# Perceiver kernel on one core: biases added to x ahead, a shorter last layernorm, fewer count matmuls, logits behind each tile's transposes, last value scaling shared

## The chip, the cores and the metric

The kernel runs on one core of a Trainium2 chip. The metric is the device time of one execution in microseconds (us). All data is float32.

## The reference, cut to what matters

x has 256 rows of 512, the context 25088 rows of 512. Six residual blocks follow each other; LN is a layernorm without scale.

```python
x = x + (LN(x) @ W1.T + mean(ctx @ W2.T) + b)                  # L0 cross
x = x + windowed_causal_attention(LN(x)) @ Wo.T + bo           # L0 attention, 16 heads
x = x + moe16(LN(x))               # sigmoid scores, groups, top 4 of 16 experts + a shared one
x = x + cross_attention(LN(x), ctx) @ Wo + bo                  # L1 cross, softmax over the QUERIES
x = x + shifted_window_attention(LN(x)) @ w_o + b_o            # L1 attention, windows of 128, shift 64
# L1 FFN: top 2 of 8 experts
logits = (LN(x) @ gate_w + gate_b) / 0.9
probs  = softmax(logits where among the top 2)
out    = sum_e probs[:, e] * (gelu(LN(x) @ w1[e] + b1[e]) @ w2[e] + b2[e])
x = x + (out - mean(out)) / sqrt(var(out) + eps) * ln_g + ln_b
```

The softmax of the L1 cross attention runs over the 256 queries, so each context row has its own sum per head; the kernel divides the values V by these sums.

## The kernel before, in words

x lies in SBUF as [128 partitions, T=2 tiles, 512]. The L1 cross attention is nearly the whole time: 49 chunks of 512 context rows are turned into K and V by products of sums of blocks (L537, with sums by POOL at L523 and additions into kT and v by DVE at L559), then for each chunk and 128 rows come scores (L1021), maxima (L1030), exponentials (L1035), sums inverted (L1056), V scaled (L1062, on POOL) and attend (L1048). K and V depend only on the context, so this work also serves as fill: while the blocks before it leave TensorE idle, `early_fill` makes chunks ahead and keeps them in SBUF or sends them to HBM. The chunks are also summed for the mean of the L0 cross block.

What sets the order: instructions written as `queue << ...` keep the program's order on their engine. All others are placed by a scheduler that works with a model of times and priorities, so where an addition on DVE ends up is seen in the built program only. Tiles come from pools; a pool gives addresses, and a DMA into an address that other tiles had before waits for their last readers. SP issues most DMAs in its own order; POOL issues a few.

The names that matter:

- `norm_T` (L166): per tile of x, `norm_stats` (L154: bn_stats, bn_aggr, sqrt on ACT, reciprocal), xn (L172), four transposes on TensorE (L179), one or two copies into xT (L182, L184).
- `add_rows` (L187): a bias row block `rows[row]` is added to a result in PSUM into a tile `tmp` (L190), and then `tmp` to x (L191). Called by `project_out` (L208) for the three attention outputs, by the L0 cross block (L686) and by the last layernorm.
- L0 cross: weights `l0x_w` loaded at L670, `l0a_wo` at L671, `cmean_b` is the mean of the context, 32 matmuls at L684. L0 attention (`self_attention`, L218) loads `l0a_wqkv` at L690 and uses it at L198 and L233.
- `places_of` (L453): counts, by matmuls with a triangular matrix `low` and with `ones`, how many rows ahead chose the same expert. Called by both expert blocks.
- `all_logits` (L465): the gate's matmuls (L469), after norm_T is done with both tiles.
- L1 attention: `window_attention` (L315), with q and k (L330, copies out at L336 to L340), scores (L351), project_out (L212). The rows of biases used late are loaded at L1144 (DMA at L100).
- L1 FFN (from L1156): logits in `lg` (L1169), scaled (L1170), `rank_of`, keep, counts, the list of items (expert and up to 128 rows), whose experts' numbers reach registers by `expert_i` (L1200) and start the weights' DMAs (L1214). `run_items` (L1301) goes through 8 items and then, under an If, more. An item has 4 parts (hf) of 512 hidden units; each does 16 matmuls (L1332, two records each in the profile), gelu on ACT (L1338), and, one part later, the second product (L1312). `weights_and_rows` (L1262) makes the softmax weights, the bias rows' product (L1274, L1277) and the scatter matrices (L1282 to L1285); it is called in item 0 behind the first part's gelu.
- The last layernorm (from L1367) normalises the two tiles of y in PSUM, multiplies by ln_g, adds ln_b and x, and writes x out (L1373).

Of the kernel before, what the change touches and what calls it, by code (L numbers as in the profile page):

```python
# [9 lines left out]
F32 = mybir.dt.float32  # L10
AF = mybir.ActivationFunctionType
ALU = mybir.AluOpType
# [25 lines left out]
def perceiver_kernel(  # L38
# [32 lines left out]
    def ps_mm(shape=None):  # L71
        tile, home = take("mm", shape)
        give(home)
        return tile
# [3 lines left out]
    def ps_ac(shape=None):  # L78
        return psum.tile(shape or [P, 512], F32, tag="ac", name="ps_ac", bufs=2)
# [83 lines left out]
        nc.vector.reciprocal(rs, sd)  # L163
        return mv[:, 0:1], rs

    def norm_T(roll=0, fill=None, untransposed=None):  # L166

        xT = work.tile([P, DC, NT], F32, tag="xT", name="xT", bufs=1)
        for t in range(T):
            mean, rs = norm_stats(x[:, t, :])  # L170
            xn = work.tile([P, D], F32, tag="xn", name="xn")
            nc.vector.tensor_scalar(xn, x[:, t, :], mean, rs, ALU.subtract, ALU.mult)  # L172
            if untransposed is not None:
                untransposed.append(xn)
            if t == 0 and fill:
                fill(2)
            tp = ps_mm([P, DC, P])
            for dc in range(DC):
                queue << nc.tensor.transpose(tp[:, dc, :], xn[:, dc * P : (dc + 1) * P], ident)  # L179
            at = (t * P - roll) % NT  # L180
            first = min(P, NT - at)
            nc.vector.tensor_copy(xT[:, :, at : at + first], tp[:, :, :first])  # L182
            if first < P:
                nc.vector.tensor_copy(xT[:, :, : P - first], tp[:, :, first:])  # L184
        return xT

    def add_rows(t, ps, row):  # L187

        tmp = work.tile([P, D], F32, tag="tmp", name="tmp")
        nc.vector.tensor_add(tmp, ps, rows[row])  # L190
        nc.vector.tensor_add(x[:, t, :], x[:, t, :], tmp)  # L191

    def feature_major(res, w, xT, col, scale=None):

# [10 lines left out]
            else:  # L205
                nc.vector.tensor_scalar(res[:, fc, :], ps, b, scale, ALU.add, ALU.mult)

    def project_out(oT, w, row):  # L208
        for t in range(T):
            ps = ps_mm()  # L210
            for dc in range(DC):
                queue << nc.tensor.matmul(  # L212
                    ps, oT[:, dc, t * P : (t + 1) * P], w[:, dc, :],
                    start=dc == 0, stop=dc == DC - 1,
                )
            add_rows(t, ps, row)

    def self_attention(xT, wo, col_q, row_v, row_o, blocks, load_qkv, fill):  # L218

        with tc.tile_pool(name="sa", bufs=1) as sa:  # L220
            v = sa.tile([P, T, D], F32, name="v_sa")
            oT = sa.tile([P, DC, NT], F32, name="oT")
            qT = sa.tile([P, DC, NT], F32, name="qT_sa")
            kT = sa.tile([P, DC, NT], F32, name="kT_sa")
            with tc.tile_pool(name="saw", bufs=1) as saw:
                wqkv = load_qkv(saw)
                xT = xT()
                feature_major(qT, wqkv[0], xT, col_q)
                feature_major(kT, wqkv[1], xT, col_q + 1)
                for t in range(T):  # L230
                    ps = ps_mm()
                    for dc in range(DC):
                        queue << nc.tensor.matmul(  # L233
                            ps, xT[:, dc, t * P : (t + 1) * P], wqkv[2][:, dc, :],
                            start=dc == 0, stop=dc == DC - 1,
                        )
                    nc.vector.tensor_add(v[:, t, :], ps, rows[row_v])
            with tc.tile_pool(name="sas", bufs=2) as sas:
                attention_blocks(sas, qT, kT, v, oT, blocks, fill)
            fill(1)  # L240
            project_out(oT, wo, row_o)

    def attention_blocks(sas, qT, kT, v, oT, blocks, fill):
        def weights(t, qp):
# [70 lines left out]
    def window_attention(xT, wqkv, wo, col_q, row_v, row_o):  # L315
# [6 lines left out]
        with tc.tile_pool(name="wa", bufs=1) as wa, tc.tile_pool(name="was", bufs=2) as was:  # L322
# [93 lines left out]
            for t in range(T):  # L416
                ps = ps_mm()
                for dc in range(DC):
                    queue << nc.tensor.matmul(
                        ps, xT[:, dc, t * P : (t + 1) * P], wv[:, dc, :],  # L420
                        start=dc == 0, stop=dc == DC - 1,
                    )
                nc.vector.tensor_add(v[:, t, :], ps, rows[row_v])
                for b in range(2):
                    nc.sync.dma_start(
                        out=v_swapped[b * HT : (b + 1) * HT, t, :],
                        in_=v[(1 - b) * HT : (2 - b) * HT, t, :],
                    )
            pT0 = transposed(e0)
            pT1 = transposed(e1)  # L430
            attend(0, pT0)
            attend(1, pT1)
            project_out(oT, wo, row_o)

    def rank_of(pool, vals, shape):

# [15 lines left out]

    def places_of(pool, chosen, n):  # L453

        ps = ps_mm([P, T + 1, n])
        for k, terms in enumerate((((low, 0),), ((ones, 0), (low, 1)), ((ones, 0), (ones, 1)))):
            for m, (w, t) in enumerate(terms):
                queue << nc.tensor.matmul(
                    ps[:, k, :], w, chosen[:, t, :], start=m == 0, stop=m == len(terms) - 1
                )  # L460
        count = pool.tile([P, T + 1, n], F32, name="count", bufs=1)
        nc.vector.tensor_copy(count, ps)
        return count[:, :T, :], count[:, T, :]

    def all_logits(xT, w, n):  # L465
        ps = ps_mm([P, T, n])
        for t in range(T):
            for dc in range(DC):
                queue << nc.tensor.matmul(  # L469
                    ps[:, t, :], xT[:, dc, t * P : (t + 1) * P], w[:, dc, :],  # L470
                    start=dc == 0, stop=dc == DC - 1,
                )
        return ps

    ps = ps_mm([P, P])
    queue << nc.tensor.matmul(ps, ones, low, start=True, stop=True)
# [191 lines left out]
    with tc.tile_pool(name="l0xw", bufs=1) as l0xw:  # L668
# [8 lines left out]
        nc.vector.tensor_copy(cmean_b, cmean.unsqueeze(2).to_broadcast([P, DC, P]))  # L677

        xT = norm_T()
        pss = [ps_mm() for _ in range(T)]  # L680
        for k in range(2 * DC):
            for t in range(T):
                lhsT = xT[:, k, t * P : (t + 1) * P] if k < DC else cmean_b[:, k - DC, :]
                queue << nc.tensor.matmul(pss[t], lhsT, l0x_w[:, k, :], start=k == 0, stop=k == 2 * DC - 1)  # L684
        for t in range(T):
            add_rows(t, pss[t], R_L0X_B)  # L686

    def l0a_qkv(pool):
        w = pool.tile([P, DC, 3 * D], F32, name="l0a_wqkv")
# [16 lines left out]
    NDENSE = (4 * NT) // (P + 1)  # L706
    NSPARSE = NE0 - NDENSE
    xns = []
    xT = norm_T(fill=early_fill, untransposed=xns)
    TE = [P, T, NE0]  # L710
    ps = all_logits(xT, l0g_w, NE0)

    def mini(shape, name, dtype=F32):
        return moe0.tile(shape, dtype, name=name, bufs=1)
# [207 lines left out]
    with tc.tile_pool(name="xa", bufs=2) as xa:  # L922
# [73 lines left out]
        def fill(upto):  # L996
            nonlocal done
            while done < min(upto, total):
                for _ in range(groups[done % len(groups)]):
                    next(stream)  # L1000
                done += 1

        fill(5)
        qT = xa.tile([P, DC, NT], F32, name="qT", bufs=1)
        feature_major(qT, wq, norm_T(fill=lambda n: fill(7)), C_L1X_BQ, SCALE)
        acc = [ps_ac([P, 2, NT]) for _ in range(2)]

        def restore(c):
# [47 lines left out]
            queue << nc.vector.reciprocal(rc, sm.rearrange("p q r -> p (q r)"))  # L1056
            return rc

        def scaled(c, s, rc):

            vs = xa.tile([P, D], F32, tag="vs", name="vs", bufs=3)
            queue << nc.gpsimd.tensor_mul(  # L1062
                vs.rearrange("p (h d) -> p h d", h=H),
                vs_of[c, s].rearrange("p (h d) -> p h d", h=H),
                rc.unsqueeze(2).to_broadcast([P, H, HD]),
            )
            return vs


# [47 lines left out]
                pending = ((n == 2, n == halves_of), [es, None], [c, s, sm])  # L1117
            finished(c)
        pc, ps, psm = pending[2]
        pending[1][1] = scaled(pc, ps, inverse(psm))  # L1120
        attend(*waiting.pop())
        for qp in range(2):
            attend(*pending[0], qp, *pending[1])
# [12 lines left out]
        oT = xa.tile([P, DC, NT], F32, tag="oT", name="oT", bufs=1)  # L1136
        for qp in range(2):
            queue << nc.vector.tensor_copy(oT[:, 2 * qp : 2 * qp + 2, :], acc[qp])
        project_out(oT, wo, R_L1X_BO)
    ctx_scope.close()  # L1140


# [13 lines left out]
    experts = ExitStack()  # L1156
    ep = experts.enter_context(tc.tile_pool(name="experts", bufs=2))
    xns = []
    xT = norm_T(untransposed=xns)
    y = [ps_ac() for _ in range(T)]  # L1160

    def mini(shape, name, dtype=F32):
# [1 line left out]


    TE = [P, T, NE1]
    ps = all_logits(xT, l1g_w, NE1)
    lg = mini(TE, "lg")
    nc.vector.tensor_add(lg, ps, grow[:, NE0:].unsqueeze(1).to_broadcast(TE))  # L1169
    nc.vector.tensor_scalar(lg, lg, 1.0 / 0.9, None, ALU.mult)  # L1170
    rank = rank_of(ep, lg, TE)
    keep = mini(TE, "keep")
    nc.vector.tensor_scalar(keep, rank, 2.0, None, ALU.is_lt)
# [48 lines left out]

    ex, nm, sm = mini(TE, "ex"), mini([P, T], "nm1"), mini([P, T], "sm1")
    nc.vector.tensor_reduce(nm, lg, AX.X, ALU.max, negate=True)
    for t in range(T):
        nc.scalar.activation(ex[:, t, :], lg[:, t, :], AF.Exp, bias=nm[:, t : t + 1])
    place = mini(TE, "place")
    nc.vector.scalar_tensor_tensor(
        place, before.unsqueeze(1).to_broadcast(TE), float(P), places, ALU.mult, ALU.add
# [30 lines left out]
    rows_of = mini([P, 2, 2, T, P], "rows_of")  # L1260

    def weights_and_rows():  # L1262
        nc.vector.tensor_mul(ex, ex, keep)
        nc.vector.tensor_reduce(sm, ex, AX.X, ALU.add)
        nc.vector.reciprocal(sm, sm)
# [35 lines left out]
    def run_items(which, final):  # L1301
# [21 lines left out]
        for item in which:  # L1323
# [3 lines left out]
            for hf, wt in enumerate(parts):  # L1327
# [9 lines left out]
                for fc in range(FC):  # L1337
                    nc.scalar.activation(  # L1338
                        hT[:, fc, :], ps[:, fc, :], AF.Gelu, bias=b1[:, hf * FC + fc : hf * FC + fc + 1]
                    )  # L1340
                if pending is None and which[0] == 0:
                    weights_and_rows()
                if hf == NHF - 1 and item + 1 in which:
                    xg = gathered(item + 1)
# [22 lines left out]
    for t in range(T):  # L1367
        mean, rs = norm_stats(y[t])
        yn = work.tile([P, D], F32, tag="xn", name="yn")
        nc.vector.tensor_scalar(yn, y[t], mean, rs, ALU.subtract, ALU.mult)  # L1370
        nc.vector.tensor_mul(yn, yn, rows[R_LN_G])  # L1371
        add_rows(t, yn, R_LN_B)
        nc.sync.dma_start(out=out_v[:, t, :], in_=x[:, t, :])  # L1373
    experts.close()
    ffn_scope.close()
# [73 lines left out]
```

## Time and profile before

| what | us |
|---|---|
| three runs | 2798.63, 2798.04, 2798.18; median 2798.18 |
| the profiled execution: its time | 2799.3 |
| its span | 2797.6 |
| mean granted clock of TensorE | 0.987 |
| TensorE's wait at L737 for the first experts' weights, at 344.34 | 6.28 |
| TensorE's wait at L198 for l0a_wqkv, at 220.68 | 3.39 |

In the profile a row of the timeline has its start, its length, engine, line, operation, tiles, and in brackets the idle time before it and what ended that. A row "x16" holds 16 instructions of one kind in a run. PE is TensorE, PEld its weight loads, DVE VectorE, ACT ScalarE, POOL GpSimd, SP SyncE. A row of the waits has the engine and line that waited, what it waited for, the total, the number of times and the longest. PEclk in tenths is the clock that TensorE was granted.

### The profile page before, as it was taken

To read this page: it belongs to the slowest core of one execution; us is meant where nothing else is said; L and a number is where in the kernel's file an instruction comes from. 1 tells how busy PE (TensorE), PEld (TensorE's weight loads), DVE (VectorE), ACT (ScalarE), POOL (GpSimd) and SP (SyncE) were. 2 spreads that over 40 slices of the span, in tenths; PEclk is the share of its full clock that TensorE was granted. 3 is DMA by queue.
4 is the path that set the end of the run, shared out by engine and by line. 5 is a ranking of instruction groups with operands and counts; after the bars stand their busy time and mean duration, and the time that the engine had idled before them with its cause. 6 is when DMAs were issued, how large, how long until landed. Compare 5 with 4: busy or idle time off the path is not lost. (4 is left out here: it accounts for less than half of the span.)

```text
span 2797.6 us, 57238 instructions
## 1 busy us (share of the span) xinstructions
PE 2721.9 (97%) x21502; PEld 1920.9 (69%) x21502; DVE 1721.7 (62%) x3052; ACT 1700.9 (61%) x7001; POOL 577.5 (21%) x529
## 2 busy tenths in 40 slices
PE   8998899999999999999999999999999999979997
PEld 7866777776666666666666666666666666656775
DVE  4436512267777777777777777777777777742101
ACT  6832100037877777777777778777887778831111
POOL 4321000023222223222222232222222323100000
PEclk9999999999999999999999999999999999989999
DMA  9961344421100101000101000101000100107673
GB/s 387 423 266 76 134 160 170 162 91 41 37 32 32 41 22 47 32 32 32 46 17 47 32 32 32 46 17 47 32 32 32 47 17 27 51 24 297 259 271 145
DMA packets 40869, 262.87 MB, mean 94 GB/s; under 512 B 5320, under 2 KB 8440, under 8 KB 13200
## 3 DMA queue, kind: packets, MB, share of 16 engines
q1 hardware_dynamic: 37408, 237.85, 22.6%
q0 software_dynamic: 3184, 21.33, 1.9%
q8 instruction: 175, 2.87, 0.4%
q14 instruction: 102, 0.84, 0.1%
HBM read 239.23 MB, written 19.40 MB: 92 GB/s over the span
## 5 line engine op out<-in xcount | busy, mean ns | idle before, releaser
L1035 ACT ACTIVATE e<-ps_sc,nm 128x256 f32<-128x256 f32 x3136 | 1437.8, 485 | 377.4 <-DVE nm L1030 376.9
L1030 DVE TENSOR_REDUCE nm<-ps_sc 128x2 f32<-128x512 f32 x1568 | 995.3, 686 | 358.0 <-PE ps_sc L1021 357.9
L1035 ACT ACTIVATION_READ_ACCUMULATOR e<-ps_sc,nm 128x1 f32 x3136 | 678.7, 216 | 0.0
L1048 PE MATMUL ps_ac<-e,vs 128*32 128x256 f32 x6272 | 420.7, 386 | 4.1 <-POOL vs L1062 4.1
L537 PE MATMUL ps_kv<-ts,wq 128*128 128x256 f32 x1568 | 387.1, 391 | 5.8 <-POOL ts L523 5.8
L537 PE MATMUL ps_kv<-wq,ts 128*128 128x256 f32 x1568 | 388.8, 392 | 0.0
L1062 POOL TENSOR_TENSOR vs<-v,rc 128x512 f32<-128x512 f32 x160 | 167.8, 1049 | 1016.3 <-DVE rc L1056 1016.3
L537 PEld LDWEIGHTS ps_kv<-ts,wq 128*128 128x128 f32 x1568 | 286.1, 190 | 91.1 <-issue 27.3
L537 PEld LDWEIGHTS ps_kv<-wq,ts 128*128 128x128 f32 x1568 | 287.2, 191 | 85.2 <-issue 26.5
L1021 PE MATMUL ps_sc<-qT,kT 32*128 32x256 f32 x4096 | 304.1, 401 | 1.5 <-ACT e L1035 1.3
L1048 PEld LDWEIGHTS ps_ac<-e,vs 128*32 128x32 f32 x6272 | 164.2, 109 | 202.2 <-issue 114.1
L559 DVE TENSOR_TENSOR v<-v,ps_kv 128x512 f32<-128x512 f32 x343 | 227.7, 677 | 82.6 <-PE ps_kv L537 58.1
L1021 PEld LDWEIGHTS ps_sc<-qT,kT 32*128 32x128 f32 x4096 | 191.4, 184 | 116.5 <-ACT e L1035 106.4
L537 PE MATMUL ps_kv<-wq,ct 128*128 128x256 f32 x1008 | 244.2, 385 | 0.0
L537 PE MATMUL ps_kv<-ct,wq 128*128 128x256 f32 x1008 | 242.4, 383 | 0.0
L559 DVE TENSOR_TENSOR kT<-kT,ps_kv 128x512 f32<-128x512 f32 x280 | 187.1, 681 | 68.4 <-PE ps_kv L537 58.4
L537 PEld LDWEIGHTS ps_kv<-wq,ct 128*128 128x128 f32 x1008 | 189.7, 191 | 38.2 <-ACT e L1035 12.9
L537 PEld LDWEIGHTS ps_kv<-ct,wq 128*128 128x128 f32 x1008 | 188.1, 190 | 38.1 <-ACT e L1035 12.6
L1338 ACT ACTIVATE hT<-ps_mm,b 128x128 f32<-128x128 f32 x128 | 36.6, 368 | 210.5 <-PE ps_mm L1332 157.3
L1021 PE MATMUL ps_sc<-qT,kTp 32*128 32x256 f32 x2176 | 156.9, 400 | 0.0
L523 POOL TENSOR_TENSOR ts<-ct 128x512 f32<-128x512 f32 x84 | 107.1, 1275 | 230.9 <-DMA ct<-in_ctx_dram 230.9
L1021 PEld LDWEIGHTS ps_sc<-qT,kTp 32*128 32x128 f32 x2176 | 99.6, 184 | 58.7 <-ACT e L1035 55.2
(273 smaller groups left out, 2180.2 us busy)
## 6 DMA issues: line engine op xcount, KB each, us to landing
ct<-in_ctx_dram SPq DMA_DIRECT2D x67, 1024.0 KB, 5.0
we<-in_l1e_dram SPq DMA_DIRECT2D x64, 1024.0 KB, 6.8
we<-in_l0e_dram SPq DMA_DIRECT2D x17, 1536.0 KB, 8.1
cs<-in_ctx_dram SPq DMA_DIRECT2D x17, 1024.0 KB, 14.6
we0o<-in_l0e_dram SPq DMA_DIRECT2D x17, 768.0 KB, 4.5
kv<-kT POOLq DMA_DIRECT2D x9, 1024.0 KB, 9.7
kv<-v POOLq DMA_DIRECT2D x9, 1024.0 KB, 9.4
vp<-kv SPq DMA_DIRECT2D x9, 1024.0 KB, 4.8
```

The costliest lines, as they stand in the source:

```text
L523: queue << nc.gpsimd.tensor_sub(ts[:, k], a, b)
L537: queue << nc.tensor.matmul(ps[:, m, :], fixed[:, d, m * P : (m + 1) * P], moving[:, d, :], start=d == 0, stop=d == 1,)
L559: queue << nc.vector.tensor_tensor(to, old, ps, ALU.subtract if a == W_A22 else ALU.add)
L1021: queue << nc.tensor.matmul(sc[r][:, i, :], kTs[c][part, 2 * qp + i, s * P : (s + 1) * P], qT[part, 2 * qp + i, :], start=True, stop=True,)
L1030: queue << nc.vector.tensor_reduce(nm[:, 2 * qp : 2 * qp + 2, r], sc[r], AX.X, ALU.max, negate=True)
L1035: queue << nc.scalar.activation(e[:, 4 * i + r, :], sc[r][:, i, :], AF.Exp, bias=nm[:, q, r : r + 1], accum_out=sm[:, q, r : r + 1],)
L1048: queue << nc.tensor.matmul(acc[qp][32 * r : 32 * r + 32, i, :], v[:, h * HD : (h + 1) * HD], es[qp][:, 4 * i + r, :], start=first and i = ...
L1062: queue << nc.gpsimd.tensor_mul(vs.rearrange("p (h d) -> p h d", h=H), vs_of[c, s].rearrange("p (h d) -> p h d", h=H), rc.unsqueeze(2).to_ ...
L1338: nc.scalar.activation(hT[:, fc, :], ps[:, fc, :], AF.Gelu, bias=b1[:, hf * FC + fc : hf * FC + fc + 1])
```

## The change

Bias rows are added to x on their own, each as soon as x's old value has been read (`add_row`), and project_out and the L0 cross block add the result in PSUM to x directly; `tmp` is gone. The last layernorm is two operations a tile. The counts take two matmuls with both tiles side by side, and two additions. In the L1 FFN the gate's matmuls of a tile stand behind that tile's transposes, the factor 1/0.9 moves from the logits into the exponential and its maximum, and `weights_and_rows`, which adds ln_b to x as well, is called behind the gelu of item 0's second part. The last of the value scalings is divided by heads between DVE and POOL.

```diff
-    def norm_T(roll=0, fill=None, untransposed=None):
+    def norm_T(roll=0, fill=None, untransposed=None, then=None):
...
+            if then is not None:
+                then(xT, t)
         return xT
 
-    def add_rows(t, ps, row):
-
-        tmp = work.tile([P, D], F32, tag="tmp", name="tmp")
-        nc.vector.tensor_add(tmp, ps, rows[row])
-        nc.vector.tensor_add(x[:, t, :], x[:, t, :], tmp)
+    def add_row(row):
+
+        for t in range(T):
+            nc.vector.tensor_add(x[:, t, :], x[:, t, :], rows[row])
...
-    def project_out(oT, w, row):
+    def project_out(oT, w):
...
-            add_rows(t, ps, row)
+            nc.vector.tensor_add(x[:, t, :], x[:, t, :], ps)
...
                     nc.vector.tensor_add(v[:, t, :], ps, rows[row_v])
+            add_row(row_o)
...
+            add_row(row_o)
             pT0 = transposed(e0)
             pT1 = transposed(e1)
             attend(0, pT0)
             attend(1, pT1)
-            project_out(oT, wo, row_o)
+            project_out(oT, wo)
...
-        ps = ps_mm([P, T + 1, n])
-        for k, terms in enumerate((((low, 0),), ((ones, 0), (low, 1)), ((ones, 0), (ones, 1)))):
-            for m, (w, t) in enumerate(terms):
-                queue << nc.tensor.matmul(
-                    ps[:, k, :], w, chosen[:, t, :], start=m == 0, stop=m == len(terms) - 1
-                )
-        count = pool.tile([P, T + 1, n], F32, name="count", bufs=1)
+        ps = ps_mm([P, 2, T, n])
+        for k, w in enumerate((low, ones)):
+            queue << nc.tensor.matmul(ps[:, k], w, chosen, start=True, stop=True)
+        count = pool.tile([P, 2, T, n], F32, name="count", bufs=1)
         nc.vector.tensor_copy(count, ps)
-        return count[:, :T, :], count[:, T, :]
+        place, total = count[:, 0], pool.tile([P, n], F32, name="total", bufs=1)
+        assert T == 2
+        nc.vector.tensor_add(total, count[:, 1, 0, :], count[:, 1, 1, :])
+        nc.vector.tensor_add(place[:, 1, :], place[:, 1, :], count[:, 1, 0, :])
+        return place, total
...
         xT = norm_T()
+        add_row(R_L0X_B)
...
-            add_rows(t, pss[t], R_L0X_B)
+            nc.vector.tensor_add(x[:, t, :], x[:, t, :], pss[t])
...
         feature_major(qT, wq, norm_T(fill=lambda n: fill(7)), C_L1X_BQ, SCALE)
+        add_row(R_L1X_BO)
...
-        def scaled(c, s, rc):
+        def scaled(c, s, rc, engines=(nc.gpsimd,)):
 
             vs = xa.tile([P, D], F32, tag="vs", name="vs", bufs=3)
-            queue << nc.gpsimd.tensor_mul(
-                vs.rearrange("p (h d) -> p h d", h=H),
-                vs_of[c, s].rearrange("p (h d) -> p h d", h=H),
-                rc.unsqueeze(2).to_broadcast([P, H, HD]),
-            )
+            n = H // len(engines)
+            for k, engine in enumerate(engines):
+                heads = slice(k * n, (k + 1) * n)
+                queue << engine.tensor_mul(
+                    vs.rearrange("p (h d) -> p h d", h=H)[:, heads],
+                    vs_of[c, s].rearrange("p (h d) -> p h d", h=H)[:, heads],
+                    rc[:, heads].unsqueeze(2).to_broadcast([P, n, HD]),
+                )
             return vs
...
-        pending[1][1] = scaled(pc, ps, inverse(psm))
+        pending[1][1] = scaled(pc, ps, inverse(psm), engines=(nc.vector, nc.gpsimd))
...
-    xT = norm_T(untransposed=xns)
+    ps, make = logits(l1g_w, NE1)
+    xT = norm_T(untransposed=xns, then=make)
...
-    ps = all_logits(xT, l1g_w, NE1)
     lg = mini(TE, "lg")
     nc.vector.tensor_add(lg, ps, grow[:, NE0:].unsqueeze(1).to_broadcast(TE))
-    nc.vector.tensor_scalar(lg, lg, 1.0 / 0.9, None, ALU.mult)
...
     nc.vector.tensor_reduce(nm, lg, AX.X, ALU.max, negate=True)
+    nc.vector.tensor_scalar(nm, nm, 1.0 / 0.9, None, ALU.mult)
     for t in range(T):
-        nc.scalar.activation(ex[:, t, :], lg[:, t, :], AF.Exp, bias=nm[:, t : t + 1])
+        nc.scalar.activation(ex[:, t, :], lg[:, t, :], AF.Exp, bias=nm[:, t : t + 1], scale=1.0 / 0.9)
...
     def weights_and_rows():
+        add_row(R_LN_B)
...
-                if pending is None and which[0] == 0:
+                if item == 0 and hf == 1:
                     weights_and_rows()
...
-        nc.vector.tensor_scalar(yn, y[t], mean, rs, ALU.subtract, ALU.mult)
-        nc.vector.tensor_mul(yn, yn, rows[R_LN_G])
-        add_rows(t, yn, R_LN_B)
+        nc.vector.scalar_tensor_tensor(yn, y[t], mean, rows[R_LN_G], ALU.subtract, ALU.mult)
+        nc.vector.scalar_tensor_tensor(x[:, t, :], yn, rs, x[:, t, :], ALU.mult, ALU.add)
         nc.sync.dma_start(out=out_v[:, t, :], in_=x[:, t, :])
```

`logits(w, n)` makes the PSUM tile and returns with it a function `make(xT, t)` with one tile's four matmuls of `all_logits`; in the L0 block it is called for both tiles behind `norm_T`, as before.

## The prediction

> **What bounds the kernel now.** I read the page's engine shares and slices first, then the PE rows of the waits, then the timeline around each stall.
>
> ```profile
> PE 2721.9 (97%) x21502; PEld 1920.9 (69%) x21502; DVE 1721.7 (62%) x3052; ACT 1700.9 (61%) x7001; POOL 577.5 (21%) x529
> ...
> PE   8998899999999999999999999999999999979997
> ...
> PEclk9999999999999999999999999999999999989999
> ```
>
> TensorE is busy 97% of the span. Asked by stretches, it is busy for 150 of 150 us in 850 to 1000 and for all of 1000 to 2400, where the change touches nothing: the built order of every engine and its waits are the same there before and after. What the change can win lies in the other 76 us, where TensorE stands still or runs at a lower granted clock, and in the tail after its last matmul. PE's waits:
>
> ```profile
> PE ps_mm L179 <- DVE xn L172: 6.7, 3, 2.5
> PE ps_mm L476 <- POOL low L128: 6.1, 1, 6.1
> PE ps_kv L537 <- POOL ts L523: 5.8, 2, 5.4
> PE ps_mm L684 <- issue: 5.3, 1, 5.3
> PE ps_ac L1048 <- POOL vs L1062: 4.1, 1, 4.1
> ```
>
> The columns are total, times, longest. The first, fourth and fifth are touched. The fourth names no releaser, so I asked the timeline and SP's own waits:
>
> ```profile
> SPq L670 <- PE ps_kv L537: 19.4, 1, 19.4
> ```
>
> ```profile
> 185.06 0.33 SPq L670 DMA_DIRECT2D l0x_w<-in_l0x_w_dram  x1
> ...
> 192.81 9.83 PE L684 MATMUL ps_mm<-l0x_w,xT 128*128 128x512 f32 x16 [5.28 <-issue]
> ...
> 202.47 7.03 PE L684 MATMUL ps_mm<-l0x_w,cmean_b 128*128 128x512 f32 x16
> ```
>
> The weights of the first projection are asked for at 185.06, after SP has waited 19.4 us for a matmul on the memory they go to. By the DMA issues (2048 KB, 7.5 us to landing) they are there at 192.56, and TensorE starts at 192.81. The two groups of 16 are alike, yet the first takes 2.8 us more: the granted clock is 0.50 in 192 to 198.
>
> **The change, part by part.** All against the profiled run: 2799.3 us, span 2797.6. The median of the runs is 2798.18, 1.1 lower; I apply the difference to it.
>
> *The tile tmp goes.* Its two buffers of 2 KB a partition free room, so addresses move. In the built order, l0x_w's DMA stands behind the last cs load, ahead of l0a_wo (issued at 151.35), and has no wait at all. At the 423 GB/s of that stretch its 2 MB take 5.0 us and land near 165. TensorE can then start L684 once xT is copied: the copies run from 187.29 to 188.57, so at about 188.3 instead of 192.81, −4.5. The idle before it is then about 0.8 us, the clock should hold, and the first group takes 7.0 instead of 9.8: −2.8. Together −7.3. Cover: the two ct loads behind it land at about 176 instead of 171; POOL reads them at about 180.65. Without those 5 us of slack the price would be up to 5. The next load, l0a_wqkv (L690), still waits for the last L684 matmul and takes 11.0 us, so TensorE's 3.39 us wait at 220.68 stays. The clock held there; moved to another moment it may not (the same loss, 2.8, at an estimated chance of 1 in 7): +0.4.
>
> *Biases ahead.* project_out makes one addition per tile from PSUM instead of two operations; ten separate additions of 0.69 on DVE take their place. The first two come at about 25 us, behind the first fill's additions on DVE; they wait for the first rows, issued by POOL at 6.38 and landed at about 14.4, so nothing stands behind them. Those of L0 attention and L1 cross attention fall among fill work, where TensorE has queued matmuls and DVE is busy 62% of the span: 0 for all six (up to 0.7 each where a full PSUM ring makes TensorE wait). In window attention they stand ahead of the first qT_wa on DVE, which was idle 3.87 us before it: 0. They do wait for the rows' DMA there (last rival). R_LN_B's two sit inside the FFN norm and are counted there.
>
> *Counts.* Five matmuls become two; an f32 matmul shows as two records, so ten become four. For L0 (L458, 329.87 to 331.06) six at 0.12 are −0.7, and two more DVE additions at 0.2 are +0.4. They lead through expert_i to the experts' weights, for which TensorE waits 6.28 us at 344.34; the clock's phase after that wait is unknown: −0.3, between −1 and +0.7.
>
> *Last value scaling shared.*
>
> ```profile
> 2450.15 0.25 DVE L1056 RECIPROCAL rc<-sm 128x16 f32<-128x16 f32 x1 [2.29 <-ACT e L1035]
> 2450.57 1.05 POOL L1062 TENSOR_TENSOR vs<-v,rc 128x512 f32<-128x512 f32 x1 [4.99 <-DVE rc L1056]
> 2451.68 3.31 PE L1048 MATMUL ps_ac<-e,vs 128*32 128x256 f32 x32 [4.05 <-POOL vs L1062]
> ```
>
> DVE's half, 256 wide, takes 0.42 by the row of L367; it starts behind rc at 2450.43 and TensorE, whose first 16 matmuls wait for that half alone, starts at 2450.9: −0.8. POOL's half is wanted 1.6 us later. The Trainium skill's page "SBUF — State Buffer", section "Who interferes with whom", speaks against sharing: a DVE operation with two SBUF inputs and a GpSimd operation that reads SBUF exclude each other for a whole instruction. By the 1.05 row halved, POOL first would put DVE's end near 2451.5, −0.2; DVE first costs nothing, since POOL's half is then ready at about 2451.4. No row shows the pair; DVE has no semaphore to cross, so I take −0.8 and keep −0.2.
>
> *L1A norm.* One addition instead of two per tile and a serial order: xT is ready about 0.15 sooner at the old clock. The clock had fallen after the 2.54 us idle before 2464.80 (0.53 in 2465 to 2472), which costs about 2 us. The skill's page "TensorE: Matmul & The Clock Gate", "HAM oscillation — how this bites in real kernels", asks only that idle gaps stay under about 3.4 us. By the rule this stage's gap, 2.9 at most, would leave the clock up, −3; by the row, 2.54 was enough, while 3.39 at 220.68 was not. The rows differ by phase, so the rule doesn't decide it: −1.0, between −0.15 and −3.
>
> *FFN norm, logits, counts.*
>
> ```profile
> 2511.11 3.42 PE L469 MATMUL ps_mm<-l1g_w,xT 128*128 128x8 f32 x16
> ...
> 2514.57 0.17 DVE L1169 TENSOR_TENSOR lg<-ps_mm,grow 128x16 f32<-128x16 f32 x1 [2.52 <-PE ps_mm L469]
> 2514.78 0.17 DVE L1170 TENSOR_SCALAR lg<-lg 128x16 f32<-128x16 f32 x1
> ```
>
> DVE's new order is x0, norm 0, x1, bias 0, xT0, norm 1, bias 1, xT1. With the row durations x1 ends at 2506.1, bias 0 at 2506.7, xT0 at 2507.3, xn1 at 2509.3, xT1 at 2511.1 (old 2512.0). Half of the logits (1.7) now runs behind tile 0, so lg comes at about 2513.1: −1.5 at half clock, up to −2.7 at full; I take −1.9. The bias additions cost 0.6 of that. L1170 goes: −0.15. Counts at half clock: six records at about 0.22 are −1.3, two small additions +0.3. All leads through expert_i to the first weights: −3.1.
>
> *Weights and rows behind the second half.* This goes the other way. In before TensorE fills 2530.93 to 2536.15 with L1274, L1277 and L1284; then the second half's matmuls start. Now these come first and wait for their weights. The DMAs of item 0 were issued from 2522.10; the first two land at 2527.2 and 2530.3, the third at 2533.6. TensorE is done with the first half at 2531.1: it stands 2.5 us, and the moved work, no longer a cover, comes later in full. Both times shift alike with the start: +2.5 (1.5 to 4 with a clock drop).
>
> *Tail.*
>
> ```profile
> 2788.99 0.81 DVE L1370 TENSOR_SCALAR yn<-ps_ac,bn_mv,bn_rs 128x512 f32<-128x512 f32 x1
> ...
> 2793.69 0.69 DVE L191 TENSOR_TENSOR x<-x,tmp 128x512 f32<-128x512 f32 x1
> ```
>
> Eight operations between these rows become four, all on DVE. Starting after the second bn_aggr at 2788.57: two from PSUM at 0.75 pitch (L757's), two reciprocals, two at 0.61: the last ends near 2791.8 instead of 2794.38, −2.5. The output's DMA follows as before.
>
> Sum: −7.3 + 0.4 − 0.3 − 0.8 − 1.0 − 3.1 + 2.5 − 2.5 = −12.1, so 2798.18 − 12.1 = 2786.1. The profiled run would then be 2787.2.
>
> **The rivals.**
> - *The clock holds at both late boundaries* (L1A norm −3 instead of −1, logits −2.7 instead of −1.9, attend −1.6 instead of −0.8): 3.6 less, 2782.5. For it: shorter gaps. Against: 2.54 us already let it fall. 14%.
> - *The late gains are eaten*: L1A norm wins 0.15, logits 1.5, item 0 costs 4 and the clock falls at l0a_wqkv: 0.85 + 0.4 + 1.5 + 2.4 = 5.2 more, 2791.3. For it: each has its row above. Against: their phases are independent. 13%.
> - *The early load doesn't do what it says*: l0x_w lands early, but TensorE's restart is held by something else that was hidden behind the 5.28 us, or by late ct loads. The 7.3 are gone, 2793.4. For it: nothing shows what else is due in 188 to 192. Against: xT and cmean_b are done at 188.57. 8%.
> - *Slower*: the bias additions of window attention wait for the rows' DMA, issued at 2462.71, landing in 4.9 us, and stand ahead of qT_wa on DVE. TensorE wants qT_wa for L351 at 2476.80; the two additions (1.2) and qT_wa itself (0.5) leave until 2475.1. Every us after that costs one: the 12.1 are eaten at a landing 24.5 us behind the issue, and at 28 the kernel takes 2798.18 − 12.1 + 15.6 = 2801.7. The DMA queues are nearly empty there (share 0.29). 4%.
>
> The likeliest has 61%, with its own range 2783.5 to 2789.0. About 0.2% (5.6 us) is what a measurement here can tell from no change: faster means under 2792.6. The likeliest and the first two rivals lie there, 0.88 less a little at the edge: 0.87; the third is within 0.2%, 0.09 with that edge; 0.04 are slower. The range, 2781.8 to 2791.8, takes in both clock cases and leaves out the last two.
>
> **What would show it.** L684 begins within 1.5 us of the last transposes and its two groups take 7.0 each; SP's wait for ps_kv is gone. lg comes about 2 us sooner after L212's end. A new idle of about 2.5 us stands before the 17th to 32nd L1332 matmul of item 0, released by a weights' DMA. From the first bn_st to the last x is 4.8 us instead of 7.3. It is wrong if L684 still idles, if the main phase 850 to 2400 changes its length, or if qT_wa waits for rows.

## The result and the profile after

Changed kernel: 2792.07 us, median of 18 runs (2789.16 to 2798.62); before 2798.16 (18 runs). The ratio is 0.9979, interval 0.9972 to 0.9986: faster by 0.2%, half of the 12.1 us forecast, and 0.3 us outside the range. The profiled run took 2791.85, its span is 2790.1.

Two of the lines shown of before, from the page of the changed kernel:

```profile
PE 2717.9 (97%) x21490; PEld 1923.3 (69%) x21490; DVE 1722.4 (62%) x3055; ACT 1698.8 (61%) x7001; POOL 576.9 (21%) x529
...
PEclk9999899999999999999999999999999999999999
```

Of TensorE's waits in the changed kernel (total, times, longest):

```profile
PE ps_mm L199 <- DMA l0a_wqkv<-in_l0a_wqkv_dram: 4.2, 1, 4.2
...
PE ps_mm L475 <- DVE xT L182: 3.4, 3, 1.5
PE ps_ac L1059 <- DVE vs L1076: 3.4, 1, 3.4
...
PE ps_mm L1347 <- DMA we<-in_l1e_dram: 2.5, 1, 2.5
```

The 5.3 us of L684 (now L692) are gone, the attend waits 0.7 less, and the forecast wait for item 0's second weights is there (2.5). Two rows were not forecast: the wait for l0a_wqkv is 0.8 longer than its 3.4, and the logits (L475) wait 3.4 in three places.

The first gain and what came of it, in the timeline of TensorE:

```profile
188.29 7.13 PE L692 MATMUL ps_mm<-l0x_w,xT 128*128 128x512 f32 x16 [0.51 <-DVE xT L182]
195.26 7.03 PE L692 MATMUL ps_mm<-l0x_w,cmean_b 128*128 128x512 f32 x16
...
214.29 15.54 PE L199 MATMUL ps_mm<-xT,l0a_wqkv 128*128 128x256 f32 x64 [4.22 <-DMA l0a_wqkv<-in_l0a_wqkv_dram]
```

Start and both groups are as forecast to about 0.1 us: at L692's end 7.22 us are won. Then TensorE waits for l0a_wqkv, and the clock falls there. The same row of before:

```profile
220.68 14.05 PE L198 MATMUL ps_mm<-xT,l0a_wqkv 128*128 128x256 f32 x64 [3.39 <-DMA l0a_wqkv<-in_l0a_wqkv_dram]
```

The granted clock in the changed kernel (a row has from and to, the length, then the busy time of TensorE, of its weight loads, of DVE, ACT and POOL; the third number from the end is the clock):

```profile
214.00:217.00 3.00, 2.71 (x7) 2.21 (x8) 0.00 (x0) 0.00 (x0) 0.00 (x0) 0.50 0.23 98
217.00:221.00 4.00, 4.00 (x19) 3.55 (x18) 0.97 (x2) 0.00 (x0) 0.00 (x0) 0.96 0.00 0
```

By the end of L234 4.90 us are left: the wait took 0.8 more, and the group behind it 1.5 more (15.54 instead of 14.05). Lined up by TensorE's milestones, the two profiled executions differ so:

| up to | gain so far | the step alone |
|---|---|---|
| end of L692 (L0 cross) | 7.22 | 7.2 |
| end of L234 (v of L0 attention) | 4.90 | −2.3 |
| end of L0's counts | 3.28 | −1.6 |
| end of the L0 experts | 2.39 | −0.9 |
| last attend's end | 4.79 | 2.4 |
| start of L1A's q and k | 5.60 | 0.8 |
| first L1347 of item 0 | 8.74 | 3.1 |
| first L1327 of item 0 | 4.43 | −4.3 |
| last x | 7.44 | 3.0 |

I use one more number. The trace holds the stretches of half clock; for each I take half of TensorE's busy time in it as the time lost, an estimate. Before: 23.4 us, span less this 2774.2. After: 21.2 and 2769.0. So by this estimate the profiles differ by 5.2 of direct work and 2.2 of clock. It is rough: two profiles of the changed kernel differ by 1.1 in the span less lost time (e12), and those of e13 and e18, which differ in the place of one tile, by 4.9 (2771.9 and 2776.8).

### The profile page after: what moved, and what is told of

Read it like the earlier page. It is cut to its first block, busy times and chain, and to the rows that moved or that the text cites. A ratio compares the mean times of both kernels' runs of the same rounds, so it can differ in the third digit from the quotient of the medians.

```text
span 2790.1 us, 57216 instructions
## 1 busy us (share of the span) xinstructions
PE 2717.9 (97%) x21490; PEld 1923.3 (69%) x21490; DVE 1722.4 (62%) x3055; ACT 1698.8 (61%) x7001; POOL 576.9 (21%) x529
## 5 line engine op out<-in xcount | busy, mean ns | idle before, releaser
L1076 POOL TENSOR_TENSOR vs<-v,rc 128x512 f32<-128x512 f32 (+1 forms) x160 | 167.4, 1046 | 1016.5 <-DVE rc L1067 1016.5
```

The source lines that it names most:

```text
L1076: queue << engine.tensor_mul(vs.rearrange("p (h d) -> p h d", h=H)[:, heads], vs_of[c, s].rearrange("p (h d) -> p h d", h=H)[:, heads], rc ...
```

## The experiments

Two theories. **C**: each direct gain is there, but the half clock that ought to go with a removed wait comes back at another place, and new short waits bring more. **B**, the rival: the early load is worth little, its 2 MB only delay other loads. Later **D**: the falls have nothing to do with what TensorE does; **O**: a direct cost was overlooked; **P**: the prediction's own sum; **W**, a form of O: a wait at L0's logits was overlooked. Times are medians; the numbers in brackets are the ratio to the kernel before, timed beside each run, and its 95% interval. The ratio is not made from the medians (in e11 the two are 1.5 us apart). The medians of before are 2797.9 to 2798.8, and an interval reaches 2 us or more to each side: two medians that differ by less than about 3 are not told apart, and there only the profiles speak, mostly one of each kernel.

### Early weights: e1_room_back, e3_before_no_tmp

e1, on the changed kernel:

```diff
+    for _ in range(2):
+        room = work.tile([P, D], F32, tag="tmp", name="tmp")
+        nc.vector.memset(room[:, :1], 0.0)
```

> The changed kernel with the 4 KB a partition of tmp taken again and not used, so that l0x_w's DMA waits for the last ps_kv matmul as in the kernel before. Theory C (each direct gain is there, and part of it is handed back where the granted clock falls at another moment): L692 starts about 4.5 us later and runs its first group in about 9.8 us; up to the end of the L234 group the net loss is 4 to 5.5 us, because TensorE's wait for l0a_wqkv goes back to about 3.4 and the clock holds there; the time is 2795 to 2798. Rival B (the early load is worth little, its 2 MB only delay other loads): within 2 us of the changed kernel, 2790 to 2794.

e3, on the kernel before:

```diff
-        tmp = work.tile([P, D], F32, tag="tmp", name="tmp")
-        nc.vector.tensor_add(tmp, ps, rows[row])
-        nc.vector.tensor_add(x[:, t, :], x[:, t, :], tmp)
+        nc.vector.tensor_add(x[:, t, :], x[:, t, :], ps)
+        nc.vector.tensor_add(x[:, t, :], x[:, t, :], rows[row])
```

> The kernel before with tmp alone gone: the bias and the result are each added to x directly, still behind the matmuls, two operations as before. l0x_w's DMA is free of waits. Theory C: L684 starts 4.5 us earlier, 7.2 us are won by its end, 4 to 7 of them remain at the end of the L233 group; the time is 2791.5 to 2794.5. Rival B: 2796 to 2798.5.

e1: 2796.71 (0.9994, 0.9985 to 1.0003), 4.6 more than the changed kernel. e3: 2794.10 (0.9984, 0.9975 to 0.9993), 4.1 less than before. B falls: 4 KB a partition that nobody fills are worth 4 to 4.6 us. But 6.9 had been forecast. TensorE's wait for l0a_wqkv is 2.6 to 3.4 in the profiles without the bias additions there (before, e3, e9, e10) and 3.6 to 4.4 in those with them (the changed kernel, e1, e2, e11, e12): its growth goes with the additions, not with the early load. In both profiles the clock falls there (half clock from 222.8 and 213.1), as it does in the changed kernel; before it had not, with 3.39 us of idle.

The kept profiles say when it falls. In each, the stretches of half clock begin on a grid of 3.41 us. Of the 20 profiles 14 have this wait with neither unread matmuls (e5, e7, e15, e16) nor thirds (e4, e6), and the clock fell in nine: in all those where TensorE stood idle for 2.01 us or more within one step of the grid, and in none of the other five (1.96 at most). The length of the wait does not decide it: 2.80 us were enough in e9, 3.77 were not in e8, whose wait is divided between two steps. The steps of e8, and then the steps of e9 with one of half clock behind them:

```profile
207.61:211.02 3.41, 1.60 (x12) 1.24 (x10) 2.62 (x5) 0.00 (x0) 1.40 (x2) 1.00 1.04 346
211.02:214.44 3.42, 1.45 (x7) 1.33 (x8) 0.00 (x0) 0.00 (x0) 0.00 (x0) 1.00 0.73 307
```

```profile
214.00:217.41 3.41, 2.67 (x17) 2.17 (x15) 2.60 (x6) 0.00 (x0) 3.08 (x3) 1.00 1.02 440
217.41:220.82 3.41, 1.36 (x6) 1.25 (x7) 0.38 (x1) 0.00 (x0) 0.00 (x0) 1.00 0.78 317
220.82:224.23 3.41, 3.41 (x9) 2.69 (x8) 0.48 (x1) 0.00 (x0) 0.00 (x0) 0.50 0.03 12
```

An estimate from this: a wait of 3.4 us keeps the clock only if an edge of the grid lies in its middle 0.6 us, and one of over 4 us never does. If every position of the grid is as likely, the chance of a fall is about 0.8, not 1 in 7.

### Item 0: e2_first_part

```diff
-                if item == 0 and hf == 1:
+                if pending is None and which[0] == 0:
                     weights_and_rows()
```

> The changed kernel with weights_and_rows behind the first part of item 0 again. Theory C: the 2.5 us wait for the second part's weights goes, and so does the clock's fall that followed it, about 1.7: 4.3 us less, about 2788. Rival B (the moved work is hidden, what was lost between the counts and the first L1327 lies in slower expert loads): within 1 us of the changed kernel, 2791 to 2793.

2789.66 (0.9965, 0.9953 to 0.9978), 2.4 less than the changed kernel. With the lost time taken out, from the counts' end to the first L1327 the changed kernel's profile is 2.9 longer than before and e2's equal to it within 0.1. In the changed kernel:

```profile
2518.55 3.81 PE L1347 MATMUL ps_mm<-xg,we 128*128 128x128 f32 x32 [1.04 <-DVE g L1259]
2524.88 5.36 PE L1347 MATMUL ps_mm<-xg,we 128*128 128x128 f32 x32 [2.52 <-DMA we<-in_l1e_dram]
```

The second part's matmuls take 5.36 instead of 3.81: behind 2.52 us of idle the clock fell. Wait 2.5, clock 1.6. C had forecast both, 4.3 less, and the median has 2.4: in e2's own profile the clock falls ahead of the first part, whose matmuls take 5.37. By the medians alone (intervals that overlap) the gain would not be shown.

### l0a_wqkv in thirds: e4_qkv_thirds

```diff
-        nc.sync.dma_start(out=w, in_=l0a_wqkv_d)
-        return [w[:, :, k * D : (k + 1) * D] for k in range(3)]
+        parts = [slice(k * D, (k + 1) * D) for k in range(3)]
+        for part in parts:
+            nc.sync.dma_start(out=w[:, :, part], in_=l0a_wqkv_d[:, :, part])
+        return [w[:, :, part] for part in parts]
```

> The changed kernel with l0a_wqkv loaded by three DMAs, q, k and v one behind the other. Theory C: the first 1 MB lands about 6 to 7 us behind the issue at 202.4, before TensorE wants it at 210.07, so the 4.2 us wait and the half clock behind it (1.5) go: 5 to 6 us less, about 2786.5; where the clock falls later instead, 3 to 4 less. Rival B (the wait is for bandwidth shared with POOL's kv store, all three thirds progress together): 0 to 1.5 less.

2784.49 (0.9954, 0.9940 to 0.9968), 7.6 less than the changed kernel and more than C's 5 to 6. The wait falls from 4.22 to 1.22 and no half clock follows:

```profile
210.79 5.42 PE L199 MATMUL ps_mm<-xT,l0a_wqkv 128*128 128x256 f32 x24 [1.22 <-issue]
```

So the wait gives 3.0, and the half clock behind it 1.5 more. The profile's lost time is 17.0 instead of 21.2, so 2.7 of the 4.2 lie at other places; that they are due to the edit is not shown. The rival of shared bandwidth (0 to 1.5 less) falls.

### Does the clock follow TensorE's work? e5_warm, e12_again

e5 leaves all work in place and adds matmuls whose result is not used, at six places of the changed kernel; the first:

```diff
+    def warm(n):
+        ps = ps_mm([P, NE0 * NE0])
+        for _ in range(n):
+            queue << nc.tensor.matmul(ps, ident, tri.rearrange("p a b -> p (a b)"), start=True, stop=True)
...
                 xT = xT()
+                warm(8)
                 feature_major(qT, wqkv[0], xT, col_q)
```

> The changed kernel with matmuls that nobody reads (tri by ident, 128x256, about 0.43 us each at full clock) put where TensorE stands still: 8 ahead of the q product of L0 attention, 12 ahead of the first experts' weights, 5 ahead of the last attend, 3 ahead of the counts of L1 FFN, 6 ahead of its first gather, 4 ahead of item 0's second part. No real work is taken away. Theory C (the clock falls after stretches with little TensorE work, and the half-speed work that follows is what ate the gains): the stretches of half clock at these places go or get shorter, the TensorE time lost to them sinks from about 21 us to 12 to 15, and the time is 2784 to 2788. Rival D (the falls come by themselves and have nothing to do with what TensorE does): the time stays or rises, 2791 to 2796.

2787.27 (0.9961, 0.9947 to 0.9974), 4.8 less than the changed kernel. Lost time 16.1 instead of 21.2; span less lost time 2769.0, the changed kernel's to 0.1. At l0a_wqkv, where the clock had been 0.50 behind the wait:

```profile
210.00:214.00 4.00, 3.23 (x15) 2.56 (x14) 0.39 (x1) 0.00 (x0) 0.00 (x0) 1.00 0.84 309
214.00:217.00 3.00, 3.00 (x15) 2.66 (x14) 0.48 (x1) 0.00 (x0) 0.00 (x0) 1.00 0.05 19
```

D falls: more TensorE work made the kernel faster, and in this profile all of it came from the clock.

e12 is the changed kernel unaltered, profiled again.

> The changed kernel unaltered, for a second profile of it. Theory C with windows that run free of the program: the stretches of half clock begin at other moments than in the first profile and TensorE loses another sum to them, by 1 to 4 us, while the span less this sum is the same within 1.5 us. Rival (the falls are tied to the program's places): the same stretches within 0.5 us.

One run, 2790.69. Its half clock lies elsewhere: where the first profile had 0.50 for the six microseconds behind L0's logits, this has

```profile
310.00:316.00 6.00, 6.00 (x29) 5.28 (x29) 4.77 (x19) 2.09 (x3) 0.00 (x0) 1.00 0.00 0
```

and around 213 it has 6.8 us of half clock instead of 3.4. Lost 21.1; span less this 2767.9. C's guess of a different sum was off (21.1 against 21.2), its different places were right. The stretches start on a grid of 3.41 us in each profile, at another moment of the program in each.

### The shared scaling: e8_pool_alone

```diff
-        pending[1][1] = scaled(pc, ps, inverse(psm), engines=(nc.vector, nc.gpsimd))
+        pending[1][1] = scaled(pc, ps, inverse(psm))
```

> The changed kernel with the last value scaling on POOL alone, as before. Theory C: TensorE's last attend starts 0.7 later, and where the clock falls in that stretch 1 to 1.4 more: 0.7 to 2 more than the changed kernel, about 2793. Rival (the shared halves exclude each other, so nothing was won): the same as the changed kernel within 0.3 in the profile from the last rc to the first attend.

2793.99 (0.9986, 0.9976 to 0.9996), 1.9 more. The last attend waits 4.05 instead of 3.36: 0.7 direct. The rest of the 1.9 is not told from chance; e8's runs lie between 2788.4 and 2800.4. In the changed kernel:

```profile
2447.78 0.42 DVE L1076 TENSOR_TENSOR vs<-v,rc 128x256 f32<-128x256 f32 x1
2447.84 0.83 POOL L1076 TENSOR_TENSOR vs<-v,rc 128x256 f32<-128x256 f32 x1 [4.97 <-DVE rc L1067]
```

POOL's half took 0.83 where half of its 1.05 would be 0.53: that fits standing until DVE was done at 2448.20, as the Trainium skill's page "SBUF — State Buffer" ("Who interferes with whom") has it for such a pair. DVE came first, so nobody waited for it.

### Single parts on the kernel before: e9, e10, e11

e9 takes from the change the logits, the counts and the moved factor alone; e10 the last layernorm in two operations with ln_b added ahead; e11 the other four biases ahead, with project_out's one addition.

> The kernel before with the logits behind each tile's transposes, the two count matmuls and the moved factor alone. Theory C: in the profile the way from L1A's last matmul to the first expert weights' DMA gets about 1.5 to 2.5 us shorter with the half clock's share taken out, since item 0's order is the old one that reaches the end; the time is 2794.5 to 2797, where the clock's falls take back a part. Rival P (the prediction's own sum, 3.1 in the FFN and 0.3 in L0): 2794 to 2795.

> The kernel before with the last layernorm in two operations a tile and its ln_b added to x ahead, alone. From the first bn_st on y to the last x 4.5 us instead of 7.3, so 2.8 less there; the two additions stand in the FFN norm's chain and cost up to 0.6. Theory C: 2795.3 to 2796.2, with nothing to take it back, since TensorE is done. Rival (the output's DMA sets the end): 2797 to 2798.

> The kernel before with the four biases of L0 and L1 cross and attention added to x ahead, one addition a tile in project_out, and tmp's room kept by the last layernorm. Theory C: nothing is won at L0 and the L1X boundary, and at the L1A norm the serial order gives the shorter additions back: 2797 to 2798.5, no difference. Rival P (1.0 less at the L1A norm, more in the FFN norm): 2795.5 to 2796.8.

e9: 2799.98 (1.0008, 0.9999 to 1.0017). e10: 2794.47 (0.9988, 0.9979 to 0.9997). e11: 2800.34 (1.0002, 0.9993 to 1.0011), its runs in two heaps, 2794.6 to 2794.8 and 2798.5 to 2802.6. Only the tail's gain is clear of no change, and more than C's 2795.3 to 2796.2. The changed kernel's tail ends so:

```profile
2783.84 1.39 DVE L1385 SCALAR_TENSOR_TENSOR yn<-ps_ac,bn_mv,rows 128x512 f32<-128x512 f32 x2
...
2786.19 0.75 DVE L1386 SCALAR_TENSOR_TENSOR x<-yn,bn_rs,x 128x512 f32<-128x512 f32 x1
```

4.5 us from bn_st at 2782.41 to the end, 7.3 before. For e9 and e11 neither C's numbers nor P's were right. Once the lost time is out both profiles are shorter than before (2773.1 and 2772.3 against 2774.2), but by little more than two profiles of one kernel differ. In e11's, more is lost (26.3).

### What of it is the logits? e13 to e18

e13 is the logits with the factor alone, e14 the counts alone, e15 the kernel before with unread matmuls at five places, e16 the same with e9's part.

> The kernel before with the logits of L1 FFN behind each tile's transposes and the moved factor alone. Theory C: direct gain 0.5 to 1, and half clock that comes and goes: 2797 to 2799.5. Rival O (a direct cost was overlooked in this part): over 2799.5, with a longer way from L1A's last matmul to the counts in the profile.

> The kernel before with the two count matmuls alone. Theory C: direct gain about 0.8 in the FFN and none in L0: 2796.5 to 2798.5. Rival O (fewer records leave TensorE too little work in L0's counts and the clock falls there): 2799 to 2801, with more half clock around 330 to 345.

> The kernel before with unread matmuls at the five places of L0 attention, first experts' weights, last attend, counts and first gather (8, 12, 5, 3, 6). Theory C: TensorE loses about 5 to 9 less to half clock, so 2789 to 2794. Rival D: 2797 to 2800.

> The same with the FFN part (logits, factor, counts). Theory C: with less half clock the direct gain shows, 0.8 to 2 less than e15. Rival O (a direct cost): 1 to 2 more than e15.

e13: 2802.55 (1.0016, 1.0007 to 1.0025), all eleven runs at 2800.01 or more. e14: 2798.65 (0.9999, 0.9990 to 1.0008). e15: 2796.10 (0.9995, 0.9986 to 1.0004); e16: 2796.71 (0.9996, 0.9987 to 1.0005). C had forecast 2789 to 2794 for e15, and 0.8 to 2 less than this for e16; neither came. With unread matmuls the FFN part costs 0.6 instead of 1.8, too close to tell, and these matmuls won 1.9 here, an interval that includes no change, against 4.8 in e5. The one cost clear of no change is e13's, 4.6. In its profile 31.1 us are lost to half clock instead of 23.4, which is more than the whole of its longer span (2803.1 instead of 2797.6). A wait that nobody had seen is there as well. L0's logits in the timeline of TensorE, before and then changed:

```profile
312.48 1.96 PE L469 MATMUL ps_mm<-l0g_w,xT 128*128 128x16 f32 x16 [0.51 <-DVE xT L182]
```

```profile
308.19 2.46 PE L475 MATMUL ps_mm<-l0g_w,xT 128*128 128x16 f32 x16 [1.10 <-DVE xT L182]
```

Before, it starts behind the first copy of xT (312.43), in the changed kernel behind the second (308.14); e13 and e9 wait 1.11 too. The change takes this PSUM tile ahead of norm_T in L0 also, though the matmuls stay behind it, and in the built program the first matmul then waits for the later copy. The half clock behind it lasted 6.8 us in eight of the twelve profiles with the new order by then, and 3.4 in all five of the old one without unread matmuls. e17 undoes this in the changed kernel, e18 in e13:

```diff
-    ps, make = logits(l0g_w, NE0)
     xT = norm_T(fill=early_fill, untransposed=xns)
+    ps, make = logits(l0g_w, NE0)
```

> The changed kernel with the PSUM tile of L0's logits taken behind norm_T again, nothing else. Theory W (a wait was overlooked there, and with it half clock): the idle before the first L0 logits matmul is 0.51 instead of 1.10, the half clock there 3.4 or none instead of 6.8 in most profiles; 1.5 to 2.5 less than the changed kernel, 2789.5 to 2790.5. Rival: the falls there are chance, no difference, 2791.5 to 2793.

> The kernel before with the logits of L1 FFN behind each tile's transposes and the moved factor, with L0's logits as before. Theory W: of the 4.6 that the part cost 1.5 to 2.5 go, so 2800 to 2801; what is left is half clock in the L1 stages. Rival: all of it is L0's, 2796 to 2798; or none, 2802 to 2803.

e17: 2791.47 (0.9978, 0.9969 to 0.9987), 0.6 less than the changed kernel: the idle is 0.51 again, that is all that shows, and W's 1.5 to 2.5 in time did not come. e18: 2800.94 (1.0009, 0.9999 to 1.0018), 1.6 less than e13 and 2.2 more than before beside it, an interval that includes no change. In the profiles of e13 and e18 item 0 takes 3.3 us more from its first matmuls on, by a fall that the profile of before does not have: behind the products with 8 rows (L1277 before), with TensorE busy for 2.5 of 3 us. Two windows of e18:

```profile
2531.00:2534.00 3.00, 2.52 (x14) 1.28 (x13) 0.34 (x2) 1.14 (x4) 0.00 (x0) 1.00 1.01 421
2535.00:2541.00 6.00, 6.00 (x13) 3.00 (x12) 1.90 (x4) 0.00 (x0) 0.00 (x0) 0.50 1.01 423
```

The same work kept the clock before (1.00 in 2531 to 2536). Here too the grid decides. In six of the 20 profiles the clock fell behind this work (e5, e8, e13, e15, e17, e18), just those in which a step of the grid begins between 0.70 us ahead of the first of these products and 1.24 behind it; in the other 14 the steps begin 1.11 to 2.03 ahead. e15 has the old order, so the fall does not need the new logits. Why all eleven runs of e13 are slow is open.

### Faster versions: e6, e7

e6 is the changed kernel with e2's and e4's edits; e7 adds unread matmuls at four places.

> The changed kernel with l0a_wqkv in thirds and weights_and_rows behind the first part of item 0. Theory C: both gains add up, since neither has the other's cover: 2784.5 less 2.4 to 4.3, so 2780 to 2782.5. Rival: they share a clock fall and do not add, 2784 to 2786.

> The same with the unread matmuls ahead of the first experts' weights (12), the last attend (5), the counts (3) and the first gather (6). Theory C: another 4 to 6 less, 2775 to 2778. Rival D: no gain, 2781 to 2784.

e6: 2783.57 (0.9943, 0.9930 to 0.9957). e7: 2779.66 (0.9936, 0.9922 to 0.9949). e6 has 0.9 over e4, less than the 2.4 of e2 alone and than C's 2780 to 2782.5; with five runs each and 2778.4 to 2784.5 in e6, whether the two add up is not settled. e7 has 3.9 over e6, where C had forecast 4 to 6. e7's profile loses 9.8 us to half clock, the least of all.

## Why the prediction was wrong, point by point

The direct waits and lengths came as forecast, most of them to a few tenths. What failed is the price of the half clock: +0.4 for the fall at l0a_wqkv, and nothing for L0's logits.

- **What bounds it, and where the time lies**: right. Between 850 and 2400 nothing changed its length by more than 0.4 us.
- **tmp goes, −4.5 and −2.8, then +0.4**: the two gains were exact to 0.1 at L692's end. The step that failed is "+0.4", a loss of 2.8 at a chance of 1 in 7 that the clock falls at l0a_wqkv. It fell in nine of the 14 profiles with this wait, both of the changed kernel among them. In the changed kernel's first profile the fall took 1.5, and the wait, put at no change, was 0.8 longer: 2.3 of the 7.22 won. Of 6.9, 4.1 to 4.6 are left by the medians (e3, e1).
- **Biases ahead, 0, and L1A norm, −1.0**: the term measured −0.8 to −0.9 in the profile, and the part alone is +2.1 by the median (e11). Its interval includes no change, so the time does not judge this term.
- **Counts in L0, −0.3**: too small to tell (e14).
- **L0's logits**: not in the sum at all. I had compared the order of instructions and missed a wait that moved from the first copy to the second: 0.6 of idle (e17's profile), and nothing clear in time.
- **Scaling shared, −0.8**: 0.7 in the profile (e8); the 1.9 in time is within its uncertainty. The mechanism was right, and DVE came first, as assumed.
- **FFN norm, logits, counts, −3.1**: 3.04 in the profiled pair, and +1.8 by the median as a part alone (e9). That is 4.9 from the forecast, the largest distance of all, but with an interval that includes no change. The sum read one profile's half clock as if it belonged to the program. The way did get shorter in the pair; that half clock eats this gain is argued from e13's profile, and no run takes the clock out of it wholly.
- **Item 0, +2.5**: the wait is 2.52, and 1.6 of clock came with it, 4.1 together, at the edge of its own bounds (1.5 to 4); 2.4 in time (e2).
- **Tail, −2.5**: −2.8; with ln_b's additions −3.7 as a part alone.

In the profiled pair the misses add up to the gap: early weights 2.0 less than forecast, L0's later stages 2.8 less, item 0 1.8 worse, L1A 0.2 less, against 1.6 more won up to the last attend and 0.5 at the tail: 4.7, the distance from −12.1 to −7.45. The loss in L0's later stages is half clock, of which the second profile of the changed kernel (e12) has none behind L0's logits, so this part is in some measure the pair's luck. The medians differ by 1.4 less than this pair. The single parts by their medians (−4.1, −1.9, −3.7, +1.8, +2.1, +2.4) add to −3.4 against −6.1 together; each is uncertain by about 2.5 us, so this sum proves nothing finer. Of the rivals, "the late gains are eaten" came nearest: 2791.3, with the clock as its cause. It had l0a_wqkv and item 0 among its places; L0's logits it did not have, and the L1A and FFN gains that it gave up came in full in the pair. So its number is in part luck.

## What to carry to other kernels

Price a wait taken away as the wait alone, and the half clock around it as a sum that the kernel may spend elsewhere: a second profile of the same kernel shows how far it wanders. Ask of every moved allocation which wait it changes, not only which order. And where TensorE must stand still for three microseconds, try cutting the load it waits for, or giving it unread work: 7.6 came with a wait shortened by 3.0 (e4), 4.8 with no work taken away (e5), but on the kernel before unread matmuls won 1.9, which is not told from nothing (e15).

## What the runs showed of the hardware

- The clock fell where idle gaps were well under the 3.4 us that the Trainium skill's page "TensorE: Matmul & The Clock Gate" ("HAM oscillation — how this bites in real kernels") asks for: after 2.80 us (e9), after 2.52 us (2522.36 to 2524.88), and after one of 1.10 us between transposes and products with 16 columns. It held through 3.39 us before and 3.77 us in e8. At l0a_wqkv the measure was the idle time within one step of 3.41 us: 2.01 and more fell, 1.96 and less held, in 14 profiles. At places with transposes and small products it fell with less idle than that (0.51 in the step ahead of the fall at L0's logits, before).
- Half clock came in steps of 3.41 us and at another moment in each profile, which agrees with the free-running window of that page's section "What's actually happening". But in the middle of the program the moment is not just any: the grid's first edge lies between 0.12 and 2.89 us behind the span's start, and at L0's logits, in all 20 profiles, an edge lies between 1.04 and 2.56 us ahead of the first of these matmuls. Work at half clock up to an edge would draw the positions together so; this is not tested.
- 4 KB a partition of unused room brought a wait of 5.4 us back (e1), and without tmp it was gone (0.5 in e3).
